# A graph attention kernel: the last ten pairs of edge units in three rounds of the pipeline instead of eight

## The chip, the cores and the metric

The kernel runs on one core of a Trainium2 chip. The metric is the device time of one execution in microseconds (us), as a median over runs. The engines are PE (TensorE, matmuls and transposes; its weight loads are listed as PEld), DVE (VectorE), ACT (ScalarE), POOL (GpSimd, which here only gathers rows) and SyncE (SP, which issues nearly all other DMAs). Each engine works through its own queue in order; semaphores tie the queues together.

## The reference

One layer of a graph network on 12500 nodes with 128 features and 400000 edges, sorted by their destination. There are 8 heads of 16 channels, and every edge has 32 attributes.

```python
h = jnp.maximum(_layernorm(x, axis=-1), 0.0)
# inside the layer, x is h:
m     = leaky_relu(x_l[src] + x_r[dst] + e, 0.2)       # x_l, x_r, e: ln(x) @ W_l, ln(x) @ W_r, edge_attr @ W_e
alpha = jnp.einsum('ehc,hc->eh', m, att)
amax  = segment_max(alpha, dst)
expa  = jnp.exp(alpha - amax[dst])
denom = segment_sum(expa, dst)
a     = expa / (denom[dst] + 1e-16)
out   = segment_sum(x_l[src] * a[:, :, None], dst)      # each node also has an edge to itself
h  = x + out + bias
ff = gelu(_ln(h, ln2_g, ln2_b) @ W1 + b1) @ W2 + b2
return x_input + h + ff
```

## The kernel before

A first part computes the rows of `x_l` for all nodes and puts them in DRAM; it ends well before the stretch of interest. The rest, `window_edges`, walks over the edges in order.

**Pairs.** 256 edges make a unit, two units a *pair* (512 edges), and there are 782 pairs, 0 to 781; pair 781 has only 128 edges. A pair c goes through these steps, each a small function of c:

- `gather` (POOL): fetches the rows `xs` of the 512 sources by indirect DMA.
- `windows` (SyncE): loads edge attributes, destinations and the window `zw` of `x_r`, for some of it once in four pairs.
- `place` (DVE, L953, and L959 for every second pair): makes the one-hot rows of the destinations.
- `combine` (PE, L966 and L970): sums `x_l[src] + x_r[dst] + e` in a PSUM bank of the ring `z`.
- `slope` (ACT, L984) and `bend` (DVE, L989): the leaky relu, into `m`.
- `apart` (PE, L977) and `score` (PE, L994): scores of every edge for every node and head of the window, in a bank of the ring `ab`.
- `lowest` (DVE, L1000; L1003 for the last pair) and `weigh` (ACT, L1011): the running maximum into `rec` and the exponentials `p`.
- `turn` (PE, L1019) and `keep_turned` (ACT, L1024), "keep" below: transpose `p` in a bank of the ring `pt_ps` and copy it to `pt`.
- `collect` (PE, L1033): sums the weighted rows in a bank of the ring `acc`.
- `own_heads` (DVE, L1042 and L1048), "own" below: picks each node's own head, into `rec`.
- `put` (SyncE, L1059): stores the two units' sums to `state`, a DRAM tensor each for even and odd units. Neighbouring windows can overlap, so a put waits until the one before it in its tensor has landed. For the first pair of four it begins by loading eight addresses into registers (L895).

The rings `z`, `ab`, `pt_ps` and `acc` have two PSUM banks each, which makes all eight banks; a bank is free again when its last reader is done.

**Rounds.** The order of every engine's queue is written out by hand. In round r the step f with lateness k works on pair r - k, and the steps stand in the order of this table:

```python
stages = ((-AHEAD, gather), (LATE + 1, own_heads), (5, keep_turned), (0, combine), (2, apart), (4, turn),
          (LATE, collect), (2, score), (3, lowest), (1, slope), (1, bend), (3, weigh), (-1, place))
late_stages = ((-WAHEAD, windows), (LATE + 1, put))
```

with `AHEAD` 4, `WAHEAD` 3 and `LATE` 6: a pair is combined in round c and put in round c + 7. The late stages come last in a round; between the two stand the sums of the edge attributes and the steps of the node groups.

**Node groups.** The nodes are finished in groups of four tiles of 128. A group begins when its edges must all have been put. Its steps are the `f_` functions: `f_load` fetches rows, `f_z` (PE, L1138 and L1142), `f_bend` and `f_score` (PE, L1158) make the scores of the nodes' edges to themselves, `f_state` (L1109) loads the sums back, `f_low`, `f_exp`, `f_den` (L1187 to L1193) and `f_out` (L1200 to L1216) combine them, with the weights `wp` in a PSUM bank, `f_h` and `f_stats` (L1219 to L1234) give the residual and the norm, `f_root` and `f_scale` (ACT, L1237 and L1246) apply it, `f_turn` (PE, L1257), `up0`, `up1` (PE, L1283), `gelu0`, `gelu1` (ACT, L1298) and `f_down` (PE, L1308) are the feed forward part, and `f_store` and `f_put` (L1321 to L1328) write the result. Their PSUM banks come from `bank_of`, which takes the ring `acc` unless told otherwise. Steps with the square root or the gelu make ACT load another table (`ACT_TABLE_LOAD`), as does the return to the exponential.

The last but one group has its own table `soon`; its `f_state` falls in round 772 and its steps up to `f_put` in round 781. The last group, `end`, has `last_steps`: its loads and scores come in rounds 772 to 777 (`f_order`, a copy on ACT, in 773, `f_z` in 774, `f_bend` and `f_biases` in 775, `f_score` in 776, `f_kept`, which copies the scores to `end_sc`, in 777), its `f_state` in round 790, after the last put, and all the rest in round 791, one step behind the other.

Of the kernel before, what the change touches and what calls it, by code (L numbers as in the profile page):

```python
# [13 lines left out]
F32 = mybir.dt.float32  # L14
# [8 lines left out]
P = 128  # L23
# [14 lines left out]
QP = 4  # L38
# [107 lines left out]
def tile_gnn(  # L146
# [691 lines left out]
def window_edges(  # L838
# [12 lines left out]
    EPR = UP * U  # L851
    LATE = 6
# [4 lines left out]
    n_pr = -(-NE // KP)  # L857
# [3 lines left out]
    def tiles_of(c):  # L861

        n = min(KP, NE - c * KP)
        return [range(i, min(i + KU, n)) for i in range(0, n, KU)]
# [4 lines left out]
    with ExitStack() as es:  # L869
# [4 lines left out]
        ps2 = es.enter_context(tc.tile_pool(name="e_ps2", bufs=2, space=PSUM))  # L874
# [18 lines left out]
        def words(row, top):  # L893

            return nc.values_load_multi_w_load_instructions(  # L895
                row, engines=[SP], min_val=0, max_val=top,
                skip_runtime_bounds_check_because="the first destination of a unit with edges is a node, and nodes of padding follow the last",
            )[1]

        def rows_at(t, at, n, size):  # L900

            return t.rearrange("n f -> (n f)").bitcast(U8)[ds(at, n * size)].rearrange("(n f) -> n f", f=size)
# [146 lines left out]
                d["rec"][:, :nu, 0:CX], own[:, :nu], AX.X, OP.add  # L1049
            )  # L1050

        def put(c):
            if c % QP == 0:
                at = words(first_sb[0:1, UP * c : UP * (c + QP)], (NT * P - CW) * H * SH * 4)
                for i in range(c, min(c + QP, n_pr)):
                    pairs[i]["put"] = at[UP * (i - c) : UP * (i - c + 1)]
            for i in range(len(tiles_of(c))):
                u = UP * c + i
                nc.sync.dma_start(  # L1059
                    rows_at(state[u % 2], pairs[c]["put"][i], NW * H, SH * 4), pairs[c]["rec"][:, i, :].bitcast(U8)  # L1060
                )
# [26 lines left out]
        groups = [{"t0": t, "n": n, "ts": slice(t, t + n)} for t, n in node_groups(NT)]  # L1088
        end = groups[-1]
# [8 lines left out]
            d[name] = own_tile(d, name, lambda n: [P, n, P], F32, tag)  # L1098
            return d[name][:, 0 : d["n"]]

        def bank_of(d, name, ring="acc"):
            d[name] = ps2.tile([P, EPR], F32, name=ring)
            return d[name]

        def f_state(d):
# [28 lines left out]
        def f_z(d):  # L1134

            n, z = d["n"], bank_of(d, "z")
            for i in range(n):
                nc.tensor.matmul(  # L1138
                    z[:, i * P : (i + 1) * P], d["xl"][:, i, 0:P], ident, start=(i == 0), stop=False, is_transpose=True
                )  # L1140
            for i in range(n):
                nc.tensor.matmul(  # L1142
                    z[:, i * P : (i + 1) * P], d["xr"][:, i, :], ident, start=False, stop=(i == n - 1),
                )
# [9 lines left out]
        def f_score(d):  # L1154

            n, sc = d["n"], bank_of(d, "sc")
            for i in range(n):
                nc.tensor.matmul(  # L1158
                    sc[:, i * H : (i + 1) * H], d["m"][:, i, :], negrep[:, 0, :], start=(i == 0), stop=(i == n - 1)
                )  # L1160
# [23 lines left out]
        def f_den(d):  # L1184
            n, wt = d["n"], d["wt"]
            ws = own_tile(d, "ws", lambda n: [P, 2, n * H], F32)[:, :, 0 : n * H]
            nc.vector.tensor_mul(ws, wt[:, 0:2], d["sums"][:, :, :, C])  # L1187
            den = own_tile(d, "den", lambda n: [P, n * H], F32)[:, 0 : n * H]
            nc.vector.tensor_add(den, ws[:, 0], ws[:, 1])
            nc.vector.scalar_tensor_tensor(den, den, 1e-16, wt[:, 2], op0=OP.add, op1=OP.add)  # L1190
            nc.vector.reciprocal(den, den)
            wp = bank_of(d, "wp")[:, 0 : 3 * GN * H].rearrange("p (s t) -> p s t", s=3)[:, :, 0 : n * H]
            nc.vector.tensor_mul(wp, wt, den[:, None].to_broadcast([P, 3, n * H]))  # L1193
            d["wp"] = wp
# [85 lines left out]
        def f_up(k):  # L1280
            def up(d):
                n, u = d["n"], bank_of(d, f"u{k}")
                nc.tensor.matmul(  # L1283
                    u[:, 0 : n * P],
                    w1_sb[:, k * P : (k + 1) * P],
                    d["hT"][:, 0:n].rearrange("p t f -> p (t f)"),
                    start=True,
                    stop=True,
                )

            return up

        def f_gelu(k):
            def gelu(d):
                n = d["n"]
                if k == 0:
                    d["gel"] = own_tile(d, "gel", lambda n: [P, 2, n * P], F32, "big", 3)
                nc.scalar.activation(  # L1298
                    d["gel"][:, k, 0 : n * P], d[f"u{k}"][:, 0 : n * P], AF.Gelu, bias=cols[:, 5 + k : 6 + k]
                )  # L1300

            return gelu
# [24 lines left out]
        def f_put(d):  # L1327
# [14 lines left out]
            (3, weigh),  # L1342
            (-1, place),
        )
        late_stages = (
            (-WAHEAD, windows),
            (LATE + 1, put),
        )
        sum_stages = (
# [30 lines left out]
        up0, up1, gelu0, gelu1 = f_up(0), f_up(1), f_gelu(0), f_gelu(1)  # L1380
# [15 lines left out]
            (5, f_turn),  # L1396
            (5, f_turned),
            (6, up0),
            (6, gelu0),
            (7, up1),  # L1400
            (7, gelu1),
            (8, f_down),
            (9, f_store),
            (9, f_put),
        )
        last_steps = (
            (-18, f_load),
            (-17, f_order),
            (-16, f_z),
            (-15, f_bend),  # L1410
            (-15, f_biases),
            (-14, f_score),
            (-13, f_kept),
            (0, f_state),
            (1, f_low),
            (1, f_exp),
# [21 lines left out]
        for d, u in zip(groups, done_after(NT, n_edges)):  # L1438
            d["round"] = max(free, (u // UP if u < NUE else n_pr) + LATE + 2)
            free = d["round"] + GAP  # L1440
        end["round"] = n_pr + LATE + 2

        def in_round(r, table, groups=groups):
            for k, f in table:
                for d in groups:
                    if d["round"] + k == r:
                        f(d)
# [7 lines left out]
        assert len(xr_steps) == XR_STEPS and len(raw_steps) == RAW_STEPS  # L1455

        CLEAR = 8
        with tc.manual_schedule():
            for r in range(-AHEAD, max(last_round, groups[-1]["round"] + 18)):
                in_round(r, early, groups[:-2])  # L1460
                for late, f in stages:
                    c = r - late
                    if 0 <= c < n_pr:
                        f(c)
                for late, f in sum_stages:
                    i, off = divmod(r - late, SUM_STEP)
                    if off == 0 and 0 <= i < NL:
                        f(i)
                if r > 0 and r % CLEAR == 0 and r // CLEAR < NT // GT:
                    clear(r // CLEAR)  # L1470
                in_round(r, steps, groups[:-2])
                in_round(r, soon, groups[-2:-1])
                in_round(r, last_steps, groups[-1:])
                in_round(r, enumerate(xr_steps), qs[1:])
                in_round(r, enumerate(raw_steps), raw)
                for late, f in late_stages:
                    c = r - late
                    if 0 <= c < n_pr:
                        f(c)


# [352 lines left out]
```

## Time and profile before

| What | Value |
|---|---|
| median of three runs | 4787.51 us (4777.87 to 4787.56) |
| profiled execution | 4798.77 us, span 4796.9 us |
| mean granted TensorE clock | 0.897 |
| busy share of the span | PE 80%, PEld 50%, DVE 62%, ACT 45%, POOL 62% |
| chain that ended last | PE 61%, DVE 12%, issue 11%, another core or an unknown queue 8% |
| combine of round 772, of round 781 | start at 4705.22 us, 4755.24 us |
| last gather of POOL | ends at 4729.2 us |
| load of the sums for the last group (L1109) | issued at 4772.23 us |

A row of the timeline gives start, duration, engine, line, operation and tiles, with the number of instructions merged into it, and in brackets the idle time of the engine before it and what ended that. In the chain of work that ended last each piece gives start, duration and what it was; "issue" is time in which an engine waited for nothing that the profile shows, and "remote" or "an unknown queue" stands where it can't tell who ended a wait. SPq and the like are an engine's sequencer, which issues DMAs and waits for semaphores.

### The profile page before, as it was taken

To read this page: it belongs to the slowest core of one execution; us is meant where nothing else is said; L and a number is where in the kernel's file an instruction comes from. 1 tells how busy PE (TensorE), PEld (TensorE's weight loads), DVE (VectorE), ACT (ScalarE), POOL (GpSimd) and SP (SyncE) were. 2 spreads that over 40 slices of the span, in tenths; PEclk is the share of its full clock that TensorE was granted. 3 is DMA by queue.
4 is the path that set the end of the run, shared out by engine and by line. 5 is a ranking of instruction groups with operands and counts; after the bars stand their busy time and mean duration, and the time that the engine had idled before them with its cause. 6 is when DMAs were issued, how large, how long until landed. Compare 5 with 4: busy or idle time off the path is not lost.

```text
span 4796.9 us, 63161 instructions
## 1 busy us (share of the span) xinstructions
PE 3841.3 (80%) x18434; PEld 2388.1 (50%) x18435; DVE 2973.2 (62%) x6282; ACT 2171.5 (45%) x4746; POOL 2965.3 (62%) x3146
## 2 busy tenths in 40 slices
PE   2468888888888888887888888888888888888887
PEld 1335555555455555555555555555555555555554
DVE  3646676676666566566666566666666656656656
ACT  3624344344444445445444444444444454444444
POOL 6456666666666666666666666666666666666662
PEclk9679899898999999998999998899899999899898
DMA  6546666555544444444444444444444444444432
GB/s 156 173 112 149 156 158 150 138 133 132 130 99 95 92 94 96 87 85 89 93 90 92 96 94 92 84 95 82 93 97 91 92 89 87 92 87 83 94 79 66
DMA packets 625309, 502.69 MB, mean 105 GB/s; under 512 B 320174, under 2 KB 522013, under 8 KB 624717
## 3 DMA queue, kind: packets, MB, share of 16 engines
q1 hardware_dynamic: 524381, 281.11, 25.2%
q0 software_dynamic: 100000, 217.32, 21.5%
q8 instruction: 152, 2.49, 0.2%
q14 instruction: 200, 1.64, 0.1%
q10 hardware_dynamic: 576, 0.13, 0.0%
HBM read 432.27 MB, written 65.83 MB: 104 GB/s over the span
## 4 chain that ended last, share of the span: by engine, by line
PE 61%; DVE 12%; issue 11%; another core or an unknown queue 8%; ACT 2%; DMA 1%; POOL 1%; SPq 0%; DVEq 0%; ACTq 0%; POOLq 0%
PE acc L1033 15%; PE ab L994 13%; PE z L970 13%; PE pt_ps L1019 9%; PE z L966 7%; DVE rec L1000 2%; DVE ea L953 2%; DVE m L989 2%; DVE own L1042 2%; PE acc L1283 1%; PE acc L1308 1%; POOL xs L912 1%; ACT p L1011 1%; DVE ne L959 0%
## 5 line engine op out<-in xcount | busy, mean ns | idle before, releaser
L912 POOL DMA_INDIRECT xs<-xl_dram,src_sb x3009 | 2847.0, 946 | 1694.9 <-issue 787.9
L1011 ACT ACTIVATE p<-ab,rec 128x256 f32<-128x256 f32 x1563 | 656.0, 471 | 1179.5 <-DVE rec L1000 622.5
L1033 PE MATMUL acc<-xs,pt 128*128 128x136 f32 x6250 | 1017.3, 308 | 183.6 <-issue 131.3
L1042 DVE TENSOR_TENSOR own<-acc,diag 128x272 f32<-128x272 f32 x782 | 341.3, 436 | 1297.3 <-remote 517.6
L1033 PEld LDWEIGHTS acc<-xs,pt 128*128 128x128 f32 x6250 | 907.9, 214 | 213.1 <-issue 156.3
L970 PE MATMUL z<-ea,zw 64*128 64x512 f32 x1564 | 939.4, 681 | 37.6 <-issue 14.8
L1024 ACT COPY pt<-pt_ps 128x512 f32<-128x512 f32 x782 | 456.1, 583 | 1089.0 <-remote 463.9
L994 PE MATMUL ab<-m,negrep 128*128 128x512 f32 x1564 | 902.7, 659 | 29.8 <-issue 28.5
L966 PEld LDWEIGHTS z<-ident,xs 128*128 128x128 f32 x3125 | 401.6, 151 | 716.5 <-issue 346.8
L966 PE MATMUL z<-ident,xs 128*128 128x128 f32 x3125 | 519.5, 290 | 294.2 <-issue 86.5
L1019 PEld LDWEIGHTS pt_ps<-ident,p 128*128 128x128 f32 x3125 | 358.1, 150 | 729.1 <-issue 684.0
L1019 PE MATMUL pt_ps<-ident,p 128*128 128x128 f32 x3125 | 563.8, 306 | 87.7 <-issue 72.1
L953 DVE TENSOR_SCALAR ea<-dl,nid 32x516 f32<-32x516 bf16 x782 | 582.0, 744 | 29.4 <-DMA dl<-dc_dram 4.2
L989 DVE TENSOR_TENSOR m<-z,zs 128x512 f32<-128x512 f32 x782 | 532.9, 681 | 96.7 <-issue 45.1
L1000 DVE TENSOR_REDUCE rec<-ab 128x2 f32<-128x512 f32 x781 | 533.5, 683 | 76.7 <-remote 35.6
L984 ACT ACTIVATE zs<-z 128x512 f32<-128x512 f32 x782 | 475.4, 608 | 40.4 <-DMA ea<-in_ea_t 19.7
L977 PE MATMUL ab<-ne,farw 64*128 64x512 bf16 x782 | 319.2, 408 | 98.6 <-ACT p L1011 65.4
L1048 DVE TENSOR_REDUCE rec<-own 128x34 f32<-128x272 f32 x782 | 340.9, 436 | 26.8
L970 PEld LDWEIGHTS z<-ea,zw 64*128 64x128 f32 x1564 | 245.0, 195 | 199.5 <-issue 182.2
L994 PEld LDWEIGHTS ab<-m,negrep 128*128 128x128 f32 x1564 | 278.0, 216 | 52.0 <-issue 51.5
L285 POOL DMA_INDIRECT raw<-in_x,src_raw x116 | 115.0, 992 | 68.3 <-issue 36.6
L959 DVE TENSOR_SCALAR ne<-dl,nid 96x512 bf16<-96x512 bf16 x391 | 148.7, 380 | 13.1 <-DMA dl<-du_dram 0.7
(206 smaller groups left out, 2218.0 us busy)
## 6 DMA issues: line engine op xcount, KB each, us to landing
ea<-in_ea_t SPq DMA_DIRECT2D x392, 128.0 KB
ea_s<-in_ea_t SPq DMA_DIRECT2D x98, 512.0 KB
xs<-xl_dram,src_sb POOLq DMA_INDIRECT x3009
dl<-dc_dram SPq DMA_DIRECT2D x392, 66.0 KB
state<-rec SPq DMA_DIRECT2D x1563, 9.0 KB
state<-empty SPq DMA_DIRECT2D x28, 504.0 KB
f_st<-state SPq DMA_DIRECT2D x46, 288.0 KB
dl<-du_dram SPq DMA_DIRECT2D x392, 32.0 KB
```

Source lines behind the costliest of these rows:

```text
L912: nc.gpsimd.indirect_dma_start(out=xs[:, j, :], out_offset=None, in_=xl_dram, in_offset=bass.IndirectOffsetOnAxis(ap=src_sb[:, c * KP + j ...
L953: nc.vector.tensor_scalar(d["ea"][rs].rearrange("p (a b) -> p a b", b=OW), d["dl"][rs].rearrange("p (a b) -> p a b", b=OS)[:, :, 0:OW], ni ...
L966: nc.tensor.matmul(z[:, j * P : (j + 1) * P], d["xs"][:, j, 0:P], ident, start=(j == 0), stop=False, is_transpose=True)
L970: nc.tensor.matmul(z[:, :e], d["zw"][rs], d["ea"][rs, :e], start=False, stop=True)
L984: nc.scalar.activation(d["zs"][:, :e], d["z"][:, :e], AF.Copy, scale=SLOPE)
L989: nc.vector.tensor_tensor(d["m"][:, :e], d["z"][:, :e], d["zs"][:, :e], op=OP.max)
L994: nc.tensor.matmul(d["ab"][:, :e], negrep.rearrange("p n h -> p (n h)"), d["m"][:, :e], start=False, stop=True)
L1000: nc.vector.tensor_reduce(d["rec"][:, :, CX], d["ab"].rearrange("p (u e) -> p u e", e=U), AX.X, OP.min)
L1011: nc.scalar.activation(d["p"][:, us], d["ab"][:, us], AF.Exp, bias=d["rec"][:, i, CX:SH], scale=-1.0)
L1019: nc.tensor.transpose(d["pt_ps"][:, js], d["p"][:, js], ident)
L1024: nc.scalar.copy(d["pt"][:, :e], d["pt_ps"][:, :e])
L1033: nc.tensor.matmul(d["acc"][:, i, :], d["pt"][:, j * P : (j + 1) * P], d["xs"][:, j, :], start=(j == js[0]), stop=(j == js[-1]),)
```

## The change

Pairs 772 to 781 (from `near_end` on, the last whole group of four and two before it) leave the tables `stages` and `late_stages`, except for the steps with negative lateness (`gather`, `place`, `windows`), and follow a table of their own, `last_pairs`. In it a pair is combined, sloped and bent in round c, scored and weighed in round c + 1, turned, collected and put in round c + 2. The steps of `last_pairs` stand behind those of `stages` in a round and ahead of the groups' steps. In rounds 773 to 778 the pairs up to 771 still pass through their late steps by the old table.

`put` is split: the register load is a step `addresses` of its own, for earlier pairs one round ahead of the put. The last two groups take their banks from the ring `z` where nothing else is said. In `soon`, `up1` and `gelu1` move to the round of `up0` and `gelu0`, and the steps behind them come one round earlier. The last group's `f_state` falls in round 784 and the rest in 785; its early steps keep their rounds.

```diff
-        def put(c):
+        def addresses(c):
             if c % QP == 0:
                 at = words(first_sb[0:1, UP * c : UP * (c + QP)], (NT * P - CW) * H * SH * 4)
                 for i in range(c, min(c + QP, n_pr)):
                     pairs[i]["put"] = at[UP * (i - c) : UP * (i - c + 1)]
+
+        def put(c):
             for i in range(len(tiles_of(c))):
...
-        def bank_of(d, name, ring="acc"):
-            d[name] = ps2.tile([P, EPR], F32, name=ring)
+        def bank_of(d, name, ring=None):
+            d[name] = ps2.tile([P, EPR], F32, name=ring or ("z" if d in groups[-2:] else "acc"))
...
+        last_pairs = (
+            (1, addresses),
+            (1, apart),
+            (1, score),
+            (2, turn),
+            (0, combine),
+            (0, slope),
+            (0, bend),
+            (2, keep_turned),
+            (1, lowest),
+            (1, weigh),
+            (2, collect),
+            (2, own_heads),
+            (2, put),
+        )
         late_stages = (
             (-WAHEAD, windows),
+            (LATE, addresses),
             (LATE + 1, put),
         )
...
             (6, up0),
+            (6, up1),
             (6, gelu0),
-            (7, up1),
-            (7, gelu1),
-            (8, f_down),
-            (9, f_store),
-            (9, f_put),
+            (6, gelu1),
+            (7, f_down),
+            (8, f_store),
+            (8, f_put),
...
-            (-18, f_load),
+            (-12, f_load),
...
-        end["round"] = n_pr + LATE + 2
+        end["round"] = n_pr + 2
...
+        near_end = (n_pr - 1) // QP * QP - 2 * QP
...
                 for late, f in stages:
                     c = r - late
-                    if 0 <= c < n_pr:
+                    if 0 <= c < (n_pr if late < 0 else near_end):
                         f(c)
+                for late, f in last_pairs:
+                    if near_end <= r - late < n_pr:
+                        f(r - late)
...
                 for late, f in late_stages:
                     c = r - late
-                    if 0 <= c < n_pr:
+                    if 0 <= c < (n_pr if late < 0 else near_end):
                         f(c)
```

More of the change, by code (lines that the diff above doesn't have):

```diff
@@ L1398, in window_edges @@
             (6, up0),
+            (6, up1),
             (6, gelu0),
-            (7, up1),
-            (7, gelu1),
-            (8, f_down),
-            (9, f_store),
-            (9, f_put),
+            (6, gelu1),
+            (7, f_down),
+            (8, f_store),
+            (8, f_put),
         )
         last_steps = (
-            (-18, f_load),
[L1408 to L1413, printed above, removed]
+            (-12, f_load),
+            (-11, f_order),
+            (-10, f_z),
+            (-9, f_bend),
+            (-9, f_biases),
+            (-8, f_score),
+            (-7, f_kept),
             (0, f_state),
```

## The prediction

> **What bounds the kernel now.** I read the page first: PE is busy 80% of the span, DVE and POOL 62%, and the chain that ended last is PE for 61%. The diff leaves rounds before 770 as they are but for one register load, so the question is what bounds the last 95 us. The table by windows over that stretch comes next (columns: length, then busy time of PE, PEld, DVE, ACT, POOL, then PEclk, DMA share, GB/s).
>
> ```profile
> 4660.00:4680.00 20.00, 14.60 (x77) 9.12 (x75) 9.95 (x20) 7.84 (x21) 12.30 (x13) 0.98 0.38 74
> ...
> 4710.00:4720.00 10.00, 7.81 (x43) 4.60 (x42) 8.40 (x21) 3.72 (x8) 7.57 (x8) 1.00 0.60 130
> 4720.00:4730.00 10.00, 7.86 (x37) 5.52 (x37) 9.59 (x24) 3.57 (x7) 4.73 (x5) 0.83 0.23 47
> 4730.00:4740.00 10.00, 7.65 (x45) 5.07 (x45) 7.42 (x18) 7.06 (x13) 0.00 (x0) 1.00 0.25 58
> 4740.00:4750.00 10.00, 10.00 (x53) 6.08 (x51) 7.01 (x13) 8.65 (x13) 0.00 (x0) 1.00 0.04 5
> 4750.00:4760.00 10.00, 10.00 (x67) 7.38 (x66) 7.21 (x14) 7.28 (x16) 0.00 (x0) 1.00 0.13 30
> ```
>
> The drain isn't a stretch of idle engines: from 4740 to 4760 PE has no gap at all, while the last combine (round 781) starts at 4755.24. DVE is nearly full from 4710 to 4730, where the last but one group's steps lie. Next the timeline of round 780, one pair at full clock:
>
> ```profile
> 4749.59 0.60 PE L966 MATMUL z<-ident,xs 128*128 128x128 f32 x4
> ...
> 4750.79 0.58 ACT L1024 COPY pt<-pt_ps 128x512 f32<-128x512 f32 x1
> 4751.18 0.66 PE L1019 MATMUL pt_ps<-ident,p 128*128 128x128 f32 x4
> 4751.25 0.61 ACT L984 ACTIVATE zs<-z 128x512 f32<-128x512 f32 x1
> 4751.67 1.09 PE L1033 MATMUL acc<-xs,pt 128*128 128x136 f32 x8
> ...
> 4752.60 1.02 PE L994 MATMUL ab<-m,negrep 128*128 128x512 f32 x2
> 4752.62 0.75 DVE L953 TENSOR_SCALAR ea<-dl,nid 32x516 f32<-32x516 bf16 x1
> 4753.18 0.84 ACT L1011 ACTIVATE p<-ab,rec 128x256 f32<-128x256 f32 x2
> ```
>
> From start to start this gives PE's price of a pair: combine with apart 1.59, turn 0.49, collect 0.93, score 0.86: 3.87 us. ACT: keep 0.58, slope 0.61 (starting 0.46 behind keep), weigh 0.84. DVE: place 0.75; bend 0.69, lowest 0.68, own 0.44 and its reduction 0.44 from the rows beside these. Last, the chain at the end and SyncE's own timeline:
>
> ```profile
> 4766.56 0.45 DVE own L1042
> ...
> 4767.67 1.42 DMA state<-rec
> ...
> 4769.22 1.42 DMA state<-rec
> ...
> 4770.77 1.45 DMA state<-rec
> 4772.23 0.40 SPq L1109
> ```
> ```profile
> 4757.81 0.39 SPq L1328 DMA_DIRECT2D out<-f_yo  x1
> 4758.36 12.74 SPq L1059 DMA_DIRECT2D state<-rec  x15
> ```
>
> The last puts follow each other by 1.55 us, each waiting for the one before to land; the last lands at 4772.2, although PE's last collect ended near 4766.7. The queue was late since put(774), ready at 4754.3, stood behind the group's output DMA until 4758.36. After 4772.2 comes the last group's chain to 4796.9, whose order the change leaves alone.
>
> **The change part by part.** I add up when the last put lands, against 4772.2 of this execution (4798.77 us; the three timed runs have a median of 4787.51, 11.3 less, so the difference is added to that).
>
> *A wait in every new round.* The new order on PE is apart and score of c-1, turn of c-2, combine of c, collect of c-2. ACT has slope of c, then keep of c-2. Slope waits for combine of the same round, keep stands behind slope, collect behind keep, and PE has nothing else to issue: 0.04 + 0.47 + 0.58 + 0.04 = 1.13 us of idle PE in each full round (before, slope belonged to the previous round's combine and keep came first). Behind collect the next apart and score are queued. Bend and lowest then end at about 1.4 and 2.1 us after combine, weigh at 2.95; the next turn comes up at about 3.2, so no second wait arises. Rounds 774 to 780: 7 x 1.13 = **+7.9**.
>
> *The group's burst on DVE.* f_den to f_out occupy DVE from 4717.91 to 4722.04, f_h and f_stats from 4725.13 to 4729.2, f_m and f_biases to 4730.66: 9.8 us. In eight rounds each pair has a round of slack at each step, and no PE wait in the table is put down to it. In three rounds bend of c gates score of c in the next round. I walked the queues from round 772 (4705.2) with the durations above. Round 774: apart waits for weigh(772) 1.4, turn waits for keep(769), now behind weigh(772) and the end group's 0.87 copy, 0.6. Round 775: combine waits for f_out to free the bank of wp (now in the z ring), 0.7. Round 776: collect(774) waits for a bank that own(769) frees only behind the burst, 1.4 beyond the 1.1 already counted. Round 777: collect(771) waits likewise for own(774), 1.3. Sum **+5.4**; bounds 0 (all hidden) and 9.8 (the whole burst). I take 5.4, as the walk gives it bank by bank.
>
> *Work pulled ahead of the last combine.* At combine(781) four more collects (3.7), three more turns (1.5) and two more apart and score (2.2) are done: **+7.4**, the same work as before, earlier.
>
> *Waits that go.* PE stood still 4.33 us before the end group's f_z (4717.81 to 4722.15), 2.35 in round 777 waiting for end_sc before f_turn; the matmuls from 4722 to 4726 ran at a granted clock of 0.57, costing 3.85 x 0.43 = 1.7: **-8.4**.
>
> *After the last combine.* Before: 4755.9 to 4772.2, 16.3. New: slope, keep, collect(779) 1.8; apart and score of the short last pair 0.35; wait for weigh(780) 0.8; turn 0.5; keep 0.6; collect(780) 0.95; own with reduction 0.9; two puts of 1.5 in a row 3.0: 8.9. Puts now have a round of 5 us each, so their queue is gone and f_put has no put waiting long behind it: **-7.4**.
>
> Sum so far: +4.9. *The lull.* The 4.33 us were no matter of PE's order: ACT (4.34) and POOL (2.33) waited in the same stretch for PE's semaphore, and SyncE's instructions took 0.70 in place of 0.35. Such lulls recur while POOL gathers (4663.6 to 4665.9, 4698.4 to 4700.2) and none is seen after its last gather at 4728. The new round 774 lies in that phase, so I put it back: +4.3, less the 2.0 of waits that stand at the same place: **+2.3** (bounds 0 and 4.3). Total **+7.2**.
>
> *Edits at nothing.* Both gelus in one round spare two table loads of 1.28 on ACT; before, PE was busy 10.00 of 10 us around them, and in the new order the load runs while ACT waits for lowest. [...] f_z in the z ring makes combine(771) wait for bend(770): 0 to 1.2, taken as 0, as ACT and DVE stood in a lull there. The address load (196 of them, median 0.52 us) moves ahead of the previous pair's put in SyncE's queue; behind it are puts that wait for own anyway, and 11 rec buffers cover them. put(772) stands ahead of windows(777) and put(767) on SyncE; the window isn't needed for three rounds. POOL's gathers keep their order.
>
> **The rivals.**
> *Banks in strict rotation.* My walk lets a tile take whichever bank is free first. If the oldest is taken, apart(773) waits for weigh(771), 2.5 more, apart(775) for f_h, 1.2, combine(776) for f_m, 2.1: +5.8, total +13.0, 4800.5. It decides where a bank's older reader stands behind the burst. The profile before can't tell: its rings of two never offered the choice. Chance 0.20.
> *The walk overstates the waits.* If the pairs' tighter order keeps DVE and ACT ahead (the old stages' PE work fills the gaps), the burst and half of the 1.13s vanish: 7.2 - 5.4 - 4 - 2.3 = -4.5 with the lull landing in a wait: 4783. Against it: ACT and DVE run strictly in order in every row. Chance 0.12.
> *The clock falls.* Where PE idled 4 us, the granted clock was 0.57 after; where it idled 27% in short gaps (4660 to 4680) it was 0.98. Should the short gaps of the new rounds halve it for half of their matmuls: 7 x 3.87 x 0.5 = +13.5 more, 4808. Chance 0.04. [...]
> *The address load on the path.* If a put's lateness counted in every fourth round: 196 x 0.52 = +102 us. SyncE's lateness of some us is visible in rounds 772 and 773 and delays nothing. Chance 0.02.
> *Nothing moves,* since the framework orders the queues anew: 0.02, 4787.5.
>
> **How the numbers follow.** The forecast has 0.60 and gives 4787.5 + 7.2 = 4794.7; its own range, from the bounds of lull and burst, is 4787 to 4801. A measurement of this kernel can tell about 0.2%, 9.6 us. Within that lie two thirds of the forecast's chance (0.40), a quarter of rotation's (0.05), most of the overstated walk (0.09) and the last rival (0.02): 0.56. Slower by more: 0.20 + 0.15 + 0.04 + 0.02 = 0.41. Faster: 0.03. The range reaches to the overstated walk below and past rotation above, with some us of the runs' own spread (4777.87 to 4787.56): 4782 to 4806.
>
> **What would show it.** PE idle about 1.1 us between L970 and L1033 in rounds 774 to 780, released by ACT's L1024; rounds 778 to 781 starting about 5 us apart plus the group's matmuls; the last combine near 4769 and the last put landing 9 us later; combine in round 775 released by f_out; one pair of gelu and exp loads less. Wrong if collect follows combine without a gap, if the last put lands before 4772, or if rounds before 770 take another time.

## The result: 18 us slower

The changed kernel takes 4805.14 us (median of nine runs, 4801.34 to 4810.38) where nine runs of the kernel before have 4787.51 (4777.87 to 4794.2): ratio 1.0039, interval 1.0029 to 1.0050. The forecast was 4794.7; the time lies inside its range, but the growth is 18 us and not 7.

The windows of the changed kernel's profile for the stretch that I read before (length, then busy time of PE, PEld, DVE, ACT, POOL, then PEclk, DMA share, GB/s):

```profile
4710.00:4720.00 10.00, 8.75 (x33) 6.69 (x33) 4.43 (x11) 3.30 (x8) 5.26 (x6) 0.52 0.21 51
...
4740.00:4750.00 10.00, 7.61 (x38) 4.28 (x36) 6.21 (x14) 6.59 (x12) 0.00 (x0) 1.00 0.21 41
4750.00:4760.00 10.00, 8.78 (x40) 5.79 (x41) 5.08 (x11) 6.58 (x10) 0.00 (x0) 0.91 0.13 22
```

Before, PE was busy 10.00 of 10 from 4740 to 4760 at a clock of 1.00. Now neither window is full, and the clock is 0.52 where soon's steps begin and 0.91 near the end. PE's timeline of one new round, 778, at full clock:

```profile
4743.82 1.19 PE L1033 MATMUL acc<-xs,pt 128*128 128x136 f32 x8 [1.16 <-ACT pt L1024]
...
4745.39 0.39 PE L977 MATMUL ab<-ne,farw 64*128 64x512 bf16 x1
4745.70 1.12 PE L994 MATMUL ab<-m,negrep 128*128 128x512 f32 x2
...
4747.63 1.12 PE L970 MATMUL z<-ea,zw 64*128 64x512 f32 x2
4749.98 0.38 PE L1033 MATMUL acc<-xs,pt 128*128 128x136 f32 x1 [1.22 <-ACT pt L1024]
```

The wait for keep ahead of collect is there, 1.16 and 1.22 us. The second thing to see is apart (L977): its start is 0.31 ahead of score's, and nothing runs beside it. Before, the order on PE was combine, apart, and apart ran inside L970. The rows of before, from round 780:

```profile
4750.12 0.69 PE L970 MATMUL z<-ea,zw 64*128 64x512 f32 x1
4750.13 0.39 PE L977 MATMUL ab<-ne,farw 64*128 64x512 bf16 x1
4750.65 0.59 PE L970 MATMUL z<-ea,zw 64*128 64x512 f32 x1
```

The next matmul there starts at 4751.18, 1.06 us behind the start of L970, so apart took no time of its own. From start to start the new round has apart 0.31, score 0.96, turn 0.44, L966 0.53, L970 1.12, collect 1.12 (where apart follows it directly): 4.48 us of PE work and 1.22 of wait, against 3.87 and none.

The chain at the end, to be held against the three puts of before:

```profile
4776.09 1.42 DMA state<-rec
...
4777.64 1.45 DMA state<-rec
4779.10 0.40 SPq L1111
```

Two puts in a row in place of three. From the start of the last combine to the load of the sums (L1109 before, L1111 now) it was 17.0 us and is 9.7; behind that the end group takes 24.3 where it took 24.7. The drain did what was forecast. The loss lies ahead of it.

**A ledger of the tail.** I take the stretch from the start of combine(769), the last that both kernels make in the same order, to the end, and split the time up to PE's last collect in three: PE idle; half of the PE time that lies in stretches at half clock (the matmuls would have taken half as long: from start to start those of L1033 take 0.116 us at full clock and 0.227 at half, medians of both traces of A); and the rest, PE's work at full clock. All from the traces, in us. The last columns are from a second pair of traces, both from one other chip (D, below).

| Part | before | after | forecast | measured | D before | D after | measured |
|---|---|---|---|---|---|---|---|
| PE idle up to the last collect | 10.4 | 19.8 | +8.9 | +9.4 | 6.2 | 16.5 | +10.3 |
| lost to half clock | 3.4 | 12.3 | -1.7 | +8.9 | 1.6 | 4.7 | +3.1 |
| PE's work at full clock | 66.9 | 72.6 | 0 | +5.7 | 66.5 | 73.5 | +6.9 |
| last collect to the load of the sums | 5.5 | 3.0 | 0 | -2.5 | 5.5 | 3.2 | -2.3 |
| end group | 24.7 | 24.3 | 0 | -0.4 | 24.6 | 25.4 | +0.8 |
| sum | 110.9 | 131.9 | +7.2 | +21.1 | 104.4 | 123.2 | +18.8 |

(In the forecast "work pulled ahead", +7.4, and "after the last combine", -7.4, cancel as a sum, so the rows behind the last collect are put at 0, though within it the prediction has 3.9 us from the last collect to the last put, against 5.5 before. The idle time is 7.9 + 5.4 - 4.33 - 2.35 + 2.3.) The tail grew by 21 and 19 us, the medians by 18 and 12: in both pairs the changed kernel came to combine(769) earlier, by 14.6 and 5.7 us. The profiled run of before on the first chip was 11 us above its median, which leaves some 3; on D both runs lie within 1 us of their medians. The one thing that is different ahead of round 770 is the register load, and its own run, `gelu_addr` below, gained 2.7 us of which the interval excludes neither 0 nor 6.7. That part stays open.

### The profile page after: what moved, and what is told of

Read it like the earlier page. It is cut to its first block, busy times and chain, and to the rows that moved or that the text cites. A ratio compares the mean times of both kernels' runs of the same rounds, so it can differ in the third digit from the quotient of the medians.

```text
span 4803.4 us, 63152 instructions
## 1 busy us (share of the span) xinstructions
PE 3849.3 (80%) x18434; PEld 2382.9 (50%) x18435; DVE 2974.0 (62%) x6282; ACT 2167.7 (45%) x4744; POOL 2957.2 (62%) x3146
## 5 line engine op out<-in xcount | busy, mean ns | idle before, releaser
L1033 PE MATMUL acc<-xs,pt 128*128 128x136 f32 x6250 | 1011.7, 307 | 183.4 <-issue 112.0
L1033 PEld LDWEIGHTS acc<-xs,pt 128*128 128x128 f32 x6250 | 902.6, 213 | 227.6 <-issue 147.6
L970 PE MATMUL z<-ea,zw 64*128 64x512 f32 x1564 | 943.6, 684 | 35.9 <-issue 12.3
L994 PE MATMUL ab<-m,negrep 128*128 128x512 f32 x1564 | 898.5, 657 | 25.4 <-issue 23.5
L966 PE MATMUL z<-ident,xs 128*128 128x128 f32 x3125 | 522.4, 292 | 301.2 <-issue 97.9
L966 PEld LDWEIGHTS z<-ident,xs 128*128 128x128 f32 x3125 | 401.4, 152 | 718.2 <-issue 354.1
L984 ACT ACTIVATE zs<-z 128x512 f32<-128x512 f32 x782 | 475.2, 608 | 76.6 <-PE z L970 54.2
L977 PE MATMUL ab<-ne,farw 64*128 64x512 bf16 x782 | 320.2, 409 | 100.2 <-ACT p L1011 67.4
L970 PEld LDWEIGHTS z<-ea,zw 64*128 64x128 f32 x1564 | 246.4, 196 | 199.0 <-issue 181.1
```

The lines of the kernel that those rows point to most:

```text
L966: nc.tensor.matmul(z[:, j * P : (j + 1) * P], d["xs"][:, j, 0:P], ident, start=(j == 0), stop=False, is_transpose=True)
L970: nc.tensor.matmul(z[:, :e], d["zw"][rs], d["ea"][rs, :e], start=False, stop=True)
L984: nc.scalar.activation(d["zs"][:, :e], d["z"][:, :e], AF.Copy, scale=SLOPE)
L994: nc.tensor.matmul(d["ab"][:, :e], negrep.rearrange("p n h -> p (n h)"), d["m"][:, :e], start=False, stop=True)
L1033: nc.tensor.matmul(d["acc"][:, i, :], d["pt"][:, j * P : (j + 1) * P], d["xs"][:, j, :], start=(j == js[0]), stop=(j == js[-1]),)
```

## The experiments

The kernels ran on several chips; each ratio is to runs of before on the same chip. A is the chip of the result (before: 4787.5 us; no number of it is on record, so it may be B at another time), B that of the first four experiments (4755.3), C (3980.5), D (3980.0) and E (3986.5, and 3978.9 in a second visit) the others. That the same kernel takes 17% less on C, D and E is told at the end; it makes it possible to see the change with and without the lulls.

**First four, on B: the parts by themselves.** My theories: the new round's wait is the main cost; the z ring costs where f_z holds a bank; rivals, the clock, and the number of rounds.

`keep_first`: in `last_pairs`

```diff
             (2, turn),
+            (2, keep_turned),
             (0, combine),
             (0, slope),
             (0, bend),
-            (2, keep_turned),
```

> The changed kernel with one line of last_pairs moved: keep_turned stands ahead of combine, slope and bend, so ACT copies pt of pair c-2 before it waits for combine of pair c. Theory of the order (each of the eight full new rounds pays about 1.2 us in which PE waits for slope and keep): collect follows combine without a gap, and the kernel is 8 to 10 us faster than the changed one, about 4796 us where the changed kernel took 4805. Theory of the banks (the last two groups' tiles in the z ring cost the time): no difference, 4805. Theory of the clock (PE's short waits lower the granted clock, which costs as much again): more than the waits alone, 15 us or so, back near the kernel before.

Measured: ratio 1.0020 (1.0010 to 1.0030), some 9 us less than the change has on A; the change itself was not run on B. PE's waits for keep, 10.4 us in the tail of the change on A and 9.3 on D, fall to 1.4. In the ledger PE idles 13.3 us in place of 19.8 on A, half clock costs 6.9 in place of 12.3, and the work stays dear at 74.1. The wait is real, and worth about what the forecast gave it; a loss of 8 to 10 us is left.

`z_only`: the kernel before, with the edit of `bank_of` alone.

> The kernel before with one edit of the change: the last two groups take their banks from the ring z. The eight rounds stay. Theory of the order: 0 to 2 us slower than the kernel before, since combine(771) must wait for bend(770). Theory of the banks: most of the loss shows here, 8 to 18 us slower. Theory of the clock: as the order, unless PE's wait in round 771 shows a half clock behind it.

Measured: 1.0026 (1.0015 to 1.0037), and in a later run on E, `z_only_again`, 1.0022 (1.0013 to 1.0031): 9 to 12 us for an edit that I had put at nothing.

`gelu_addr`: the kernel before, with both gelus in one round and `addresses` apart from `put`.

> The kernel before with two edits of the change: both gelus of the last but one group in one round, and the register loads of the addresses one round ahead of the put. All theories: no difference that can be measured (within 4 us), one pair of table loads less. If the address loads were on the path of the whole kernel: rounds before 770 take longer, by up to 100 us.

Measured: 0.9995 (0.9986 to 1.0004). These edits cost nothing that can be measured, as forecast.

`twice`: `near_end` three quads earlier, so that 22 pairs pass in three rounds.

> The changed kernel with twelve pairs more in three rounds: near_end at 760 instead of 772, 22 pairs instead of 10. Theory of the order: a round of last_pairs takes 5.7 us where one of the old order takes 3.9 to 4.6, so 12 more of them cost 12 to 22 us more than the changed kernel, about 4822. Theory of the banks and of the overlap with the group's burst on DVE: these come once whatever the number of pairs, so about 4805. Theory of the clock: as the order or above, with more half-clock windows from round 760 on.

Measured: 1.0116 (1.0100 to 1.0131), by medians 52.6 us over before where the change has 17.6 (on A): 35 us for twelve more pairs, above the 12 to 22 that the theory of the order expected. It is not 2.9 us for each of them. Between the starts of combine(757) and combine(781) this run takes 201.0 us and the change on A 168.3; of these 32.7 us 5.3 are PE's work, 2.1 half clock and 25.3 idle time, and three waits alone make 28.8 (PE's timeline):

```profile
4606.06 0.58 PE L977 MATMUL ab<-ne,farw 64*128 64x512 bf16 x1 [12.54 <-ACT p L1011]
...
4644.87 2.18 PE L1033 MATMUL acc<-xs,pt 128*128 128x136 f32 x8 [8.82 <-ACT pt L1024]
...
4665.48 2.18 PE L1033 MATMUL acc<-xs,pt 128*128 128x136 f32 x8 [7.45 <-ACT pt L1024]
```

In each of them ACT's slope (L984) begins 9.2, 7.7 and 6.3 us after the L970 that it follows has ended (4590.93, 4636.05, 4658.04), and the profile calls what releases it remote. These are lulls. In three rounds PE soon has nothing to do until slope and keep are through, so it stands for nearly the whole of a lull; why these last longer than the 4 to 6 us of PE's waits in the kernel before is not shown. So the cost does grow with the number of pairs, but on this chip mostly by lulls that fall into the new rounds, which no theory of this set had named. `twice` was not run on a chip without lulls.

**Four on C: f_z, apart and the number of rounds.** On A there is a place in the changed kernel where the z ring is seen to bite. Timeline of the change, all engines:

```profile
4680.84 1.06 PE L1144 MATMUL z<-ident,f_xr 128*128 128x128 f32 x8
...
4685.65 0.44 DVE L1042 TENSOR_TENSOR own<-acc,diag 128x272 f32<-128x272 f32 x1 [4.80 <-remote]
...
4687.08 0.68 DVE L989 TENSOR_TENSOR m<-z,zs 128x512 f32<-128x512 f32 x1
...
4687.86 0.66 PE L966 MATMUL z<-ident,xs 128*128 128x128 f32 x2 [5.97 <-issue]
```

f_z holds one z bank and combine(770) the other. Combine(771) (the last row) needs the bank that bend(770) frees at 4687.08 + 0.68, and bend stands in DVE's queue behind an own that a lull held for 4.80. PE has 5.97 us of nothing, and the clock is at half for the 6.8 us that follow 4686.6.

`fz_acc`: the change, with soon's f_z back in an `acc` bank (`bank_of(d, "z", "acc" if d is groups[-2] else None)`).

> The change, with one tile put back: f_z of the last but one group takes an acc bank again, its other tiles stay in the z ring. Theory of the z ring (f_z holds a z bank, so combine(771) waits for bend(770), and bend(770) stands behind a lull of DVE): combine(771) follows f_z without the 5.97 us of idle PE, and half-clock time at 4686 goes with it; 6 to 9 of the 18.6 us go, ratio to before about 1.0022. Rival, the lull (three rounds leave no slack, so any lull of 5 us is paid in full, whichever bank it meets): the idle time moves to another line of the same two rounds, ratio 1.0035 to 1.004.

Measured: 1.0030 (1.0019 to 1.0041) on C; later on E as `fz_again` 1.0032 (1.0019 to 1.0044), beside the change itself, and as `fz_third` 1.0033 (1.0020 to 1.0045). C turned out to have no lulls, so that the two theories were not told apart: there was no 5.97 to win. What the run did show is that from round 774 on its rounds have the lengths of the change on A (12.19, 9.97, 8.02, 6.09, 7.43, 9.13, 5.72 us against 12.14, 9.97, 7.99, 6.09, 7.44, 9.13, 5.72): no lull is part of them.

`ka_fz`: keep first, f_z in acc, and (0, apart) right behind (0, combine).

> The change, with three edits: keep ahead of combine in the table of the last pairs, apart of the pair before right behind combine (so that it runs beside it on the other 64 rows, as it did before the change), and f_z of the last but one group in acc. Theory of waits on PE: 9 to 11 us for keep (as its own run showed), 10 x 0.32 = 3.2 for apart, 6 to 9 for f_z: 18 to 23 of the 18.6 us go, ratio 0.999 to 1.000. Rival, the lull and the clock are paid whatever the order: only keep's and apart's parts go, ratio 1.0010 to 1.0015.

(The text speaks of apart of the pair before; the edit moves apart to the round of its own combine.) Measured: 1.0041 (1.0027 to 1.0055), no faster than `fz_acc` beside it. Keep's wait falls, and apart does run beside L970 again:

```profile
3960.21 0.69 PE L970 MATMUL z<-ea,zw 64*128 64x512 f32 x1
3960.22 0.39 PE L977 MATMUL ab<-ne,farw 64*128 64x512 bf16 x1
3960.74 0.59 PE L970 MATMUL z<-ea,zw 64*128 64x512 f32 x1
```

PE's work in the ledger is 69.8 us, against 72.4 in `fz_acc`: 2.6 of the 3.2 us expected. But a new wait took the place of the old ones (PE's timeline):

```profile
3900.19 0.58 PE L977 MATMUL ab<-ne,farw 64*128 64x512 bf16 x1 [2.77 <-ACT p L1011]
...
3911.06 0.37 PE L977 MATMUL ab<-ne,farw 64*128 64x512 bf16 x1 [2.94 <-ACT p L1011]
```

Apart one round earlier needs the `ab` bank that weigh of two pairs before still reads, and everything on PE stands behind it.

`six`: `near_end` one quad later, so that 776 to 781 alone pass in three rounds; `six_ka_fz`: the same with the edits of `ka_fz`.

> The change with six pairs (776 to 781) in three rounds instead of ten; all else as in the change, the z ring too. Theory of a price per round: a new round costs 5.72 in place of 3.87, so 4 x 1.85 = 7.4 us go, ratio 1.0024. With the 2.85 us per round that ten more rounds cost (the run with 22 pairs): 11.4 go, ratio 1.0015. Rival, the z ring and the clock are the cost and not the number of rounds: ratio 1.0035 to 1.004.

> Six pairs in three rounds, keep ahead of combine, apart right behind combine, f_z of the last but one group in acc. Theory of waits on PE: the drain's gain of 7.3 stays, six rounds cost about 0.4 each (2.4), no wait at round 771: 5 us less than before, ratio 0.999. Rival, the lull and the clock are paid whatever the order: ratio 1.0000 to 1.0010.

Measured: 1.0044 (1.0030 to 1.0057) and 1.0038 (1.0025 to 1.0052): fewer of the new rounds did not help. The six pairs share their rounds with late steps of six pairs in the old table, and rounds 776 to 780 take 45.5 us together where `fz_acc` beside it has 36.4. PE idles 18.3 us in the tail (`fz_acc`: 12.7), 3.6 of them in one wait of apart for weigh, and from the last combine to the load of the sums it takes 11.2 us and not 9.7. So a price of so much per round fails here as it does in `twice`.

**Four on D: the same chip for both, and the clock.**

> The kernel before once more, for a trace from the same chip as the next three. Its tail from the combine of pair 769 to the end took 110.9 us in the first trace, with 10.4 us of idle PE and 3.4 us lost to half clock up to the last collect. Theory of the clock gate: these stay within 3 us whatever the chip, since no round of the old order holds a wait of over 1 us that comes back in every window of the clock. Rival, the lulls set them: on a chip whose rounds before 770 run without lulls, idle PE falls under 5 us.

> The change once more, on the chip of its neighbours. Theory of the clock gate: the rounds from 774 on are as in the first trace to 0.1 us (12.1, 10.0, 8.0, 6.1, 7.4, 9.1, 5.7), with 9 us lost to half clock there, ratio to before 1.003 to 1.004. Rival, the lulls: on a chip without lulls the ratio is under 1.002.

(The window of the clock in the first text is, in the traces of A, a step of 3.41 us; see the last section.) Measured: 1.0000 (0.9991 to 1.0009) and 1.0034 (1.0022 to 1.0046). The ledger has their columns. `before_again` lost its lulls and kept 6.2 us of idle time, between the two expectations. The rounds of `after_again` are not those of A to 0.1 us (774 to 777: 9.04, 7.50, 11.68, 6.10), so the first theory's figure fell for some of them, but the ratio did not fall under 1.002: most of the loss needs no lull. The waits of PE from round 771 on, before and after on D (total us, times, longest; what was due to late gathers, 1.2 and 1.6 us, left out):

```profile
PE acc L1138 <- issue: 2.6, 1, 2.6
PE acc L1257 <- DVE end_sc L1164: 2.3, 1, 2.3
```
```profile
PE acc L1033 <- ACT pt L1024: 9.3, 9, 1.2
PE acc L1033 <- DVE own L1042: 3.2, 3, 1.9
...
PE ab L977 <- ACT p L1011: 1.4, 1, 1.4
PE z L966 <- DVE f_o L1202: 0.8, 1, 0.8
```

These are the walk's waits one by one: keep in every round, apart behind weigh(772) (1.4 forecast, 1.43 here), combine(775) behind f_out (0.7; 0.79), collect behind own (1.4 and 1.3; 0.53, 1.87 and 0.80). Up to round 780 they sum to 12.7 us; the forecast's two terms, 7.9 and 5.4, are 13.3. On A the same waits come to 10.8: keep 8.4, but of the burst only apart (1.84) and one collect (0.53).

`warm`: a second score of the pair before, right behind combine, into the bank that the next apart overwrites, so that PE works where it waits for keep; `warm_fz`: with `fz_acc` on top. In `last_pairs` (the step `again` itself and the bank that it shares with apart are left out):

```diff
             (0, combine),
+            (0, again),
...
```

> The change, and in each round from 773 on the score of the pair before is made a second time right behind combine, into the bank that the next apart overwrites: 0.96 us of matmuls whose result nobody reads, put where PE waits 1.13 to 1.22 us for keep. Theory of the clock gate (the wait of each round lets the granted clock fall to half, and the slow matmuls are what costs): the loss to half clock from 774 on falls from 9 us to 3 or less, and the kernel gains 4 to 7 us although it does more work; ratio 1.0025 to 1.003 where the change has 1.0039. Rival, the waits alone cost: the time stays or grows by up to 2 us, 1.004.

> The run before this one, and f_z of the last but one group back in an acc bank. Theory of the clock gate and the z ring as separate terms: another 6 to 9 us less where the lull before combine(771) occurs (ratio 1.001), 0 to 1 less where it doesn't. Rival, both are one and the same loss: no more than 2 us less than the run before.

Measured: 1.0044 (1.0031 to 1.0058) and 1.0051 (1.0037 to 1.0064): no gain, if anything a loss. In the ledger of `warm` the work grows from 73.5 to 81.0, idle time falls from 16.5 to 10.0, half clock goes from 4.7 to 7.2. The first fillers had waits of their own (L987 is the second score):

```profile
PE ab L987 <- ACT p L1021: 5.9, 2, 2.9
```

From 3926 on, where only 0.17 us is left of the wait in most rounds, the clock stayed at full for 44 us. In rounds 777 to 780 neither run with the filler has a stretch at half clock, while each of the six traces of the change and of `fz_acc` has one or two of 3.4 us there. (`twice`, with the same waits, has none that starts there.) So in the quiet rounds half clock went with the short waits in those six traces, and with the filler it stayed away; but there was little to win: round 779 takes 7.50 us in place of 9.14, the others are as long as before. In the rounds up to 776, where most of the loss lies, the filler's own waits spoil the test. Taken whole, the rival's line fits: the time grew.

**Four on E: another order of the same three rounds.** Still open was whether the dearer round is the order's.

`reorder`:

```diff
-            (1, apart),
-            (1, score),
             (2, turn),
+            (2, keep_turned),
             (0, combine),
+            (1, apart),
+            (1, score),
             (0, slope),
+            (1, lowest),
             (0, bend),
-            (2, keep_turned),
-            (1, lowest),
             (1, weigh),
             (2, collect),
```

> The change with another order in the table of the last pairs: turn and keep of c-2, combine of c, apart and score of c-1, slope of c, lowest of c-1, bend of c, weigh of c-1, collect of c-2. Apart again follows combine on the other 64 rows, and score stands where PE waited for keep. Theory of the dearer round (0.63 us of PE work and 1.22 us of wait in each, made by the order): PE work from combine(769) to the last collect falls from 73 to about 67 us, the wait for keep goes, a wait of 0.6 for weigh ahead of turn comes in its place; 10 x 1.25 = 12 us less than the change, ratio to before 1.000 to 1.001. Rival, three rounds leave too little slack whatever the order: other waits take the place of these, ratio 1.003 or more.

> The run before this one with f_z of the last but one group in an acc bank. Theory of the z ring: on a chip with lulls 4 to 6 us less than the run before, on one without lulls 0 to 1. Rival: no difference on either.

> The change once more, for its trace and ratio on the chip of its neighbours: 1.0034 to 1.0039 by both theories; on a chip with lulls 4 to 6 us of idle PE ahead of combine(771), on one without, under 1.

> The change with f_z of the last but one group in an acc bank, once more. Theory of the z ring: on a chip with lulls 4 to 9 us less than the change (ratio 1.0020 to 1.0030), on one without lulls within 2 us of it. Rival: within 2 us of the change on both.

Measured: `reorder` 1.0026 (1.0017 to 1.0036), `reorder_fz` 1.0023 (1.0013 to 1.0033), `after_third` 1.0031 (1.0021 to 1.0042), `fz_again` 1.0032. By medians `reorder` is 2.0 us under the change (3996.56 against 3998.58), not the 12 expected. Its tail is 114.2 us against 121.5 of `after_third`, but its profiled run was its quickest, 8 us under its median, so 7 us is too much for the others. Its rounds show what went right and what didn't. PE's timeline of one undisturbed round:

```profile
3946.24 0.60 PE L1019 MATMUL pt_ps<-ident,p 128*128 128x128 f32 x4
...
3947.21 1.12 PE L970 MATMUL z<-ea,zw 64*128 64x512 f32 x2
3948.17 0.38 PE L977 MATMUL ab<-ne,farw 64*128 64x512 bf16 x1
3948.48 1.12 PE L994 MATMUL ab<-m,negrep 128*128 128x512 f32 x2
...
3950.90 0.33 PE L1019 MATMUL pt_ps<-ident,p 128*128 128x128 f32 x1 [0.36 <-ACT p L1011]
```

4.66 us in place of 5.72: the wait for keep is gone, a wait of 0.36 for weigh came. But apart still stands alone, 0.31 from start to start, though it directly follows L970. The code says why. Even pairs place their rows in one half of the 128 partitions, odd pairs in the other, and apart multiplies the half that combine doesn't. With a lateness of 2, apart(c - 2) uses the half that combine(c) leaves free, and the trace of before has the two side by side (starts at 4750.12 and 4750.13); with a lateness of 1 both need the same 64 rows, and no order tried gave the cover back (0.31 us in the change, 0.32 in `keep_first`, 0.31 here). A lateness of 0 does, as `ka_fz` showed, at the price of its waits for an `ab` bank. The ledger agrees: 71.1 us of work, where 67 was expected. And where soon's burst is on DVE, the waits only moved (PE's waits of `reorder`):

```profile
PE acc L1033 <- DVE own L1042: 4.0, 3, 2.0
PE pt_ps L1019 <- ACT pt L1024: 2.3, 1, 2.3
PE z L966 <- DVE f_o L1202: 1.3, 1, 1.3
```

So each theory was half right: the quiet round gets cheaper by 1.06 us, those with the group's steps don't.

**Two on E: the z ring by itself.**

> The kernel before with the tiles of the last two groups in the z ring, once more. Theory (the ring costs only where a lull delays bend(770) while f_z holds the other bank): on a chip without lulls within 2 us of before, ratio 0.9995 to 1.0005, rounds 770 and 771 under 6 us each; on a chip with lulls 1.0026 as in its first run. Rival, the ring costs by itself, two banks being shared by combine and the groups' steps: 8 us or more on any chip, 1.002.

> The change with f_z of the last but one group in an acc bank, on the chip of its neighbour. Theory: on a chip with lulls ratio 1.0020 to 1.0030 and no idle PE of 4 us or more ahead of combine(771); on one without lulls 1.0030 to 1.0034, as in its two runs. Rival: 1.0035 to 1.004 on a chip with lulls.

Measured: 1.0022 (1.0013 to 1.0031) and 1.0033 (1.0020 to 1.0045). The rival holds: the ring costs by itself, 9.4 us on a chip without lulls. PE's waits of `z_only_again` in the tail:

```profile
PE z L966 <- issue: 2.6, 1, 2.6
...
PE z L1138 <- issue: 2.6, 1, 2.6
PE z L966 <- ACT f_gel L1298: 1.6, 2, 0.8
PE z L966 <- ACT f_hT L1272: 0.9, 1, 0.9
```

Every tile of a group that takes a z bank leaves combine with one bank, and combine (L966) must wait for whoever reads the other: 2.63 us right behind the end group's f_score, then f_hT and the two gelus, 0.78 to 0.87 each. The ledger has 11.9 us idle against 6.2 of before on D, and 9.9 lost to half clock against 1.6 (this profiled run was 10 us above its median, with later gathers). In the changed kernel on D these waits are not found again, but for the 0.79 behind f_out. The likely reason, not shown, is that they vanish in the 1.22 us and more that a new round waits anyway. So the ring's 9 to 12 us can't simply be added to the new rounds' cost, and on chips without lulls taking f_z alone out of it wins nothing; on a chip with lulls that was not run. Three rounds without the z ring were not tried, so how much of the change's 12 to 18 us the ring makes stays open.

No version in three rounds beats the kernel before. What a quicker drain can win at all is in the ledger: 5.5 us from the last collect to the load of the sums became 3.0, 2.5 us or 0.05%, less than can be measured.

## Why the prediction was half right

The forecast was 7.2 us of growth, and 17.6 came.

*A wait in every new round* (+7.9) and *the group's burst on DVE* (+5.4): right in place and releaser, and in size on D, 12.7 of 13.3 us; on A the first came to 8.4 and the second only to 2.4. *After the last combine*: right, 17.0 to 9.7, and two puts in a row. *Both gelus, the address load*: nothing, as said; the table loads are one gelu and one exp fewer. The lull put back at round 774 (+2.3) came at 771 instead, as 5.97 us. So the idle time on A, +9.4 where +8.9 was forecast, is right in part by luck.

**The step that failed first: "PE's price of a pair 3.87".** I took it over unchanged into the new order. It was the price of an order in which apart ran beside combine and the long ends of score and collect lay under other matmuls. Alone, they are 0.31 + 0.10 + 0.19 us more, 0.6 in each of ten rounds: 5.7 us on A, 6.9 on D, with no term in the sum.

**The second: the clock.** *Waits that go* counted 1.7 us of half clock as gained, and *The clock falls* had a chance of 0.04, on the ground that from 4660 to 4680 PE idled 27% at a clock of 0.98. That row is a mean over 20 us, while half clock comes in steps of 3.41 us (see the last section). Up to the last collect the loss was 12.3, 4.7 and 8.5 us in the three traces of the change and, for `fz_acc` three times, 9.6 us, where before had 3.4 and 1.6. So it came, at 3 to 9 us and not the rival's 13.5. The quiet rounds make little of it: of 20.5 us at half clock in `fz_acc` 17.1 lie in rounds 773 to 776, where the group's waits come on top, and the kernel before with nothing but the z ring, in eight rounds, lost 11.8 and 9.9. After a loss of 4.7 to 12.3 us in each of the three traces of the change, it deserved far more than 0.04.

**The third: "f_z in the z ring makes combine(771) wait for bend(770): 0 to 1.2, taken as 0".** On A it was 5.97 us. The reason given, that ACT and DVE stood in a lull there, was the reason against it: with one z bank PE must wait until bend is through, however long a lull holds that up. Three runs on B bear this out: `keep_first` and `z_only` have a wait of 5.8 us at the same place, and `gelu_addr`, which leaves the group in `acc` banks, has none. And the term looked at f_z alone, where the scores, f_turn and the feed forward tiles of both groups take the ring too; by itself the ring costs 9 to 12 us.

*Banks in strict rotation* gave 4800.5 and *the clock falls* 4808, with 4805 between them, by luck: the waits for banks are those of the walk and not those of rotation, and the clock is one part of the loss beside two that no rival had. *The walk overstates the waits* is refuted by the same rows for the order's own wait; of the burst a part did vanish on A.

Of the surplus over the forecast in the ledger of A, 13.9 us, 10.6 are clock, 5.7 are PE's work, and idle time and drain give back 2.4.

## What to carry to other kernels

When an order is rewritten, price its instructions anew: what ran beside something else in the old order (on other rows, under another's tail) may stand alone in the new one, and a lateness changed by one can be enough (here apart, 0.31 us in each round). A ring of two banks lent to a second user makes its first user single buffered (9 to 12 us here); list every reader that then holds it, not one. And a busy share over 10 or 20 us said little of the clock here: PE busy 73% went with 0.98 (4660 to 4680 of before), 88% with 0.52 (4710 to 4720 of the change). Look for idle time within a few us.

## What the chip showed that I had not expected

**Half clock comes in steps.** In the clock records of before and after on A the half-clock stretches start on one grid of 3.41 us, to 2 ns within a trace, and last one or more steps of it: of 171 whole stretches in before 88 last 3.41 us and 73 last 6.83, of 162 in after 71 and 82, the others longer multiples, up to 47.8. I cut both traces on that grid and looked at the step behind each. From full clock: of 1454 steps with less than 0.8 us of idle PE none was followed by half clock; with 0.8 to 1.4, 20 of 317; with 1.4 to 1.7, 58 of 129; with 1.7 or more, 256 of 336. From half clock: with under 0.2 us idle 70 of 365 steps stayed at half, with more 170 of 208. A wait of 1.22 us alone in a step is in the class with 20 of 317, with a second such wait beside it in the one with 256 of 336. Why the clock does so is not shown.

**Chips differ by 17%.** The same program, first of all the kernel before, takes 4755 to 4788 us on A and B and 3979 to 3987 on C, D and E. The head of the page of before on A, and of `before_again` on D:

```profile
PE 3841.3 (80%) x18434; PEld 2388.1 (50%) x18435; DVE 2973.2 (62%) x6282; ACT 2171.5 (45%) x4746; POOL 2965.3 (62%) x3146
```
```profile
PE 3557.0 (89%) x18434; PEld 2249.8 (57%) x18435; DVE 2998.7 (75%) x6282; ACT 2177.0 (55%) x4746; POOL 2961.6 (74%) x3146
```

DVE, ACT and POOL do the same work in the same time, to 1%. PE idles 956 us on A and 420 on D, and its busy time is 284 us longer at a mean clock of 0.897 against 0.946. The lulls (waits of 4 to 6 us, put down to "remote" or an unknown queue) are on A and B and hardly on the others: between 400 us and combine(769) PE has 43 to 55 gaps of over 3 us in the six traces of A and B, and 0 to 3 in the fourteen of C, D and E. Why some chips have them stays open. The change costs 0.39% on A, and 0.34 and 0.31% on D and E.
